# Seven half products for the eighth tile too, four matmuls handed to the next pair, and one of GpSimd's six differences as an adding transfer

## The chip, the cores and the metric

The kernel runs on one core of one Trainium2 chip. The metric is the device time of one execution in microseconds, as the median of several runs. An interval or a chance refers to that time. "The profile" is one execution recorded by the hardware profiler; its busy times, waits and timelines are of that execution alone.

## The reference

The task is a forward pass of a compressed interaction network. Three layers each form all products of two feature vectors, contract them with a weight, and hand half of the rows on.

```python
def _cin_forward(x, Ws, bs, fc_w, fc_b, split_half=True):
    x0 = x
    h = x
    xs = []
    n = len(Ws)
    for i in range(n):
        z = jnp.einsum('bfe,bge->bfge', x0, h)
        Bn, f0, fh, e = z.shape
        z = z.reshape(Bn, f0 * fh, e)
        y = jnp.einsum('oc,bce->boe', Ws[i], z) + bs[i][None, :, None]
        if split_half and i != n - 1:
            half = y.shape[1] // 2
            x_i, h = (y[:, :half, :], y[:, half:, :])
        else:
            x_i, h = (y, y)
        xs.append(x_i)
    pooled = jnp.sum(jnp.concatenate(xs, axis=1), axis=2)
    return pooled @ fc_w.T + fc_b
```

x is 1024 x 64 x 16 in float32, every layer has 128 output rows, and the result is 1024 numbers.

## The kernel before

The batch is cut into 32 chunks of 32 rows; a chunk has N = 512 columns (32 rows of 16 elements). The 64 x 64 products of a chunk are symmetric, so the kernel forms only the 16 tiles of 128 x 512 that cover each pair of features once. A block of four tiles with the same j (128 x 2048) is one product of VectorE: the chunk `xa` times a shifted copy of itself, `xb`, broadcast over the four. Fourteen such blocks, z0 to z13, are handed around by `take` and `used`: `take(uses)` takes the block that has been vacant longest, and a block becomes vacant when its uses are counted down. That happens while the program is written out, so each instruction's block is fixed, and a semaphore wait stands where a block is written again.

Each tile meets two weights of 64 columns, called h and q (`wh_all`, `wq_all`); the rest of the network is folded into them. A matmul of 64 output columns fills half the width of TensorE, so two of them, into the upper and the lower 64 partitions of PSUM, run side by side. Below, such a pair is called a row.

Chunks 6 to 31 are worked in 13 pairs (k = 3 to 15). In a pair the tiles with j = 0, 1 and those with j = 2, 3 of chunks a and b form a 2 x 2 matrix, the h and q weights of the two halves another, and their product is made by Winograd's scheme with seven half products instead of eight. The seven operands come from four kinds of blocks, each for j = 0 and 1:

- X (chunk a, low half), B21 (chunk a, high half) and B22 (chunk b, high half), which are products of VectorE in `w_product`;
- T3, a product too, of chunk b with the sum of two shifted copies, which `w_both` adds in PSUM;
- three differences that GpSimd forms in `w_mix` from these: T2 (from T3 and X), then T1, written over T3 (from B22 and T2), then T4, written over T2 (from T2 and B21). For j = 1 T2 is written over X from k = 4 on.

So there are six passes of GpSimd a pair. For j = 0 a pass covers four tiles (128 x 2048); for j = 1 it covers three (`slice(j, NI)`, 128 x 1536), because the first tile with j = 1, the eighth of each half, is left out of Winograd's scheme: `GROUPS` lacks (1, 0), each of the seven runs has seven matmuls, and the left-out tile is done with eight plain half matmuls, spread over `first_fill`, `second_fill`, `left_run` and `window`. A pair thus needs 7 x 7 + 8 = 57 half matmuls, and two more for the diagonal (`q_extra`).

`window` writes the order of TensorE's queue by hand as two columns which `zipped` interleaves: row by row one matmul of each. Column one has the X run into alpha, first fill, the T2 run, second fill, the T1 run; column two the T3 run into delta, the last pair's late run (B22 into its alpha), the B21 run into beta, the T4 run into delta. The fills hold what is left of the pair before: in `second_fill` the last one or two matmuls of its T4 run (`p["late"]`, by turns 1 and 2, 0 in the first pair). After a window come four small matmuls on 64 rows (`squares`).

The other engines' order is fixed by times in units of about a row: `make_pair` gives them for the ten VectorE operations and (`mixed`) GpSimd's six, `end_pair` for the final products of the pair before, `load_pair` for the loads on SyncE's queue. `at` collects them and everything is sorted by time at the end, so these numbers set only the order of each engine's queue; what then waits is up to semaphores. ScalarE copies the shifted chunks into PSUM (`second`), so that a VectorE product has one operand in PSUM, and keeps copies of alpha and delta (`snap_p1`, `snap_p7`, `snap_u2`) before further runs are added onto them. The run of T2 into alpha waits for `snap_p1`, and the run of T1 for `snap_u2`.

After 13 windows a final window adds the rest of the last pair and the kept chunks 2 and 3, and the sums are pooled and written out.

Of the kernel before, what the change touches and what calls it, by code (L numbers as in the profile page):

```python
# [38 lines left out]
AF = mybir.ActivationFunctionType  # L39
ALU = mybir.AluOpType  # L40
AX = mybir.AxisListType

F = 64
# [7 lines left out]
NI = 4  # L51
NJ = 4
NT = NI * NJ
# [8 lines left out]
NZ = 14  # L62
SPAN = 31
NPAIR = NCH // 2 - 3
GROUPS = [(j, i) for j in range(2) for i in range(NI) if (j, i) != (1, 0)]


@with_exitstack
def cin_kernel(ctx, tc, xra, xrb, wh, w0r, w1h, w2t, wx1, wx0, vec, out):
    nc = tc.nc  # L70
# [57 lines left out]


    w_all = const_tile("w_all", [128, NT, 128])  # L130
    ws = const_tile("ws", [128, 5, 2 * NI, F])
    va, vb, v0 = (const_tile(n, [128, F]) for n in ("va", "vb", "v0"))

    res = const_tile("res", [128, 128])
# [232 lines left out]
    for h in range(2):  # L367
        at = slice(32 * h, 32 * h + 32)
# [43 lines left out]
    for half, queue in enumerate((nc.sync, nc.scalar)):  # L412
        queue.dma_start(
            out=m_ap(0, 32 * half, [[row, F], [1, 32 * F]]), in_=m_rows[halves[half]]
# [5 lines left out]
        out=m_ap(64, 68, [[row, 4], [4 * F, 7], [1, 4 * F]]),  # L420
# [93 lines left out]
    def at(when, fn, *args, **flags):  # L514
        ops.append((when, len(ops), fn, args, flags))
# [104 lines left out]

    def w_run(p, out, w, name, start=False, at_t=0, order=GROUPS):
        return [
            (w_job, p, out, w, j * NI + i + at_t, name, start and n == 0)
            for n, (j, i) in enumerate(order)
        ]

    wh_all, wq_all = w_all[:, :, 0:64], w_all[:, :, 64:128]
    s1, s2, s3, s4, neg = (ws[:, n] for n in range(5))

    def w_product(p, c, j, name, uses, engine=nc.vector):  # L630
        p.setdefault(name, {})[j % 2] = b = take(uses)
# [6 lines left out]
        nc.vector.tensor_tensor(bank, bank, xbs[p["b"]][j], ALU.add)  # L638
        xbs[p["b"]][j] = bank

    def w_mix(p, j, out, in0, in1):
        p.setdefault(out, {})
        if j not in p[out]:
            p[out][j] = p["X"][j] if j and p["k"] > 3 else take(9 - 2 * j)
        o, x, y = p[out][j], p[in0][j], p[in1][j]
        tiles = slice(j, NI)
        nc.gpsimd.tensor_tensor(  # L647
            blocks[o][:, tiles], blocks[x][:, tiles], blocks[y][:, tiles], ALU.subtract
        )
        for b in (x, y):  # L650
            if b != o:
                used(b)
# [26 lines left out]
    def make_pair(t, p, when, mixed):  # L679
        a, b = p["a"], p["b"]  # L680
        for when, c, j, name, uses in (
            (when[0], b, 2, "B22", 5), (when[1], b, 0, None, 0), (when[2], b, 0, "T3", 9),
            (when[3], a, 0, "X", 5), (when[4], b, 3, "B22", 6), (when[5], b, 1, None, 0),
            (when[6], b, 1, "T3", 9), (when[7], a, 1, "X", 12 if p["k"] > 3 else 6), (when[8], a, 2, "B21", 5),
            (when[9], a, 3, "B21", 6),
        ):
            if name is None:
                at(t + when, w_both, p, j)
                continue
            if name == "B21" and j == 2 and p["k"] == 3:  # L690
                at(t + when, w_product, p, c, j, name, uses, engine=nc.gpsimd)
                continue
            if name != "T3":
                ahead = 3.3 if p["k"] > 4 and name == "B22" and j == 2 else 2.7
                if p["k"] == 3 and name == "X" and j == 1:
                    ahead = 9.1
                at(t + when - ahead, second, c, j)
            at(t + when, w_product, p, c, j, name, uses)
        for when, j, *names in zip(
            mixed, (0, 1, 0, 1, 0, 1), *zip(  # L700
                *(2 * (("T2", "T3", "X"),) + 2 * (("T3", "B22", "T2"),) + 2 * (("T2", "T2", "B21"),))
            )
        ):
            at(t + when, w_mix, p, j, *names)

    def first_fill(p):
        a = p["a"]
        return [
            (w_job, p, beta, wq_all, NI, "X"), (w_job, p, beta, wq_all, NT - NI, "B21"),
            (lambda: q_extra(a, va, p["beta"]),),  # L710
        ]

    def second_fill(p):
        return [
            (w_job, p, delta, wh_all, NI, "X"), (w_job, p, delta, wh_all, NT - NI, "B21"),
        ] + w_run(p, delta, neg, "T2")[7 - p["late"] :]

    def left_run(p, out, start=False):
        return [(w_job, p, out, neg, NI, "T3", start), (w_job, p, out, s4, NI, "B22")]

    def late_run(p, left=True):
        b = p["b"]
        return (left_run(p, alpha) if left else []) + w_run(p, alpha, s4, "B22") + [(lambda: q_extra(b, vb, p["alpha"]),)]

    def squares(p):
        a, b = p["a"], p["b"]
# [2 lines left out]
        v0x(b, "set")  # L729
        v0x(a, "set")  # L730

    def window(t, p, fill, late, pad=[], order=GROUPS[4:] + GROUPS[:4]):
        zipped(
            t,
            w_run(p, alpha, wq_all, "X", True, order=order) + fill[0] + w_run(p, alpha, s2, "T2")
            + fill[1] + w_run(p, alpha, s1, "T3")
            + [(w_job, p, alpha, wh_all, NI, "T3"), (w_job, p, alpha, s1, NI, "B22")],
            w_run(p, delta, s3, "T3", True) + late
            + w_run(p, beta, wq_all, "B21", True, 2 * NI)
            + pad + w_run(p, delta, neg, "T2")[: 7 - p["late"]],  # L740
        )
        at(t + 30.2, squares, p)
        at(t + 6.8, snap_p1, p)
        at(t + 6.9, snap_p7, p)
        at(t + 6.8 + len(fill[0]) + 7, snap_u2, p)

    def end_pair(t, p, whens):
        hb_, qa, uub, ha, uua, xv, add = whens
# [28 lines left out]
    def w_sums(m):  # L777
        h, q = w_all[:, 8 * m : 8 * m + 8, 0:64], w_all[:, 8 * m : 8 * m + 8, 64:128]
        if m:
            nc.gpsimd.tensor_tensor(ws[:, 3], q, ws[:, 1], ALU.subtract)  # L780
            nc.gpsimd.tensor_tensor(vb[halves[1]], va[halves[1]], w0ds[halves[1]], ALU.subtract)
            nc.scalar.activation(ws[:, 4], h, AF.Identity, scale=-1.0)
            nc.scalar.activation(ws[:, 4, NI], ws[:, 2, NI], AF.Identity, scale=-1.0)
            return
        nc.gpsimd.tensor_tensor(ws[:, 2], h, q, ALU.subtract)
        nc.gpsimd.tensor_tensor(ws[:, 1], ws[:, 0], q, ALU.add)
# [41 lines left out]
        at(34.5, factors, c)  # L828
    at(34.6, sums, 0, slice(0, 128), slice(0, 1))
    for c in (4, 5):  # L830
        at(T0 + 19.5, factors, c)
    at(T0 + 19.6, sums, 2, slice(0, 128), slice(0, 1))


    pairs = []
    for n in range(NPAIR):
        k = n + 3
        s = k % 2
        p = {
            "k": k, "A": halves[s], "O": halves[1 - s], "b": 2 * k + s, "a": 2 * k + 1 - s,  # L840
            "late": 1 + n % 2 if n else 0,
        }
        pairs.append(p)
        t = T0 + SPAN * n
        if n == 0:
            load_pair(t, p, -39.9, -33.3, -33.15, -27)
            make_pair(
                t, p, (-23.4, -20.7, -20.4, -17.8, -17.2, -16.8, -16.6, -7, -13.5, 3),
                (-14, -6.9, 7.2, 12.4, 16.4, 21.7),
            )  # L850
            left5 = [[(contract_half, 5, 3, i, n) for i in (2, 3)] for n in range(2)]
            window(
                t, p, ([left5[1][0], (q_extra, 4, va)], [left5[1][1]]),
                [left5[0][0], (q_extra, 5, va), None, None], [left5[0][1], None],
                GROUPS,
            )
        else:
            q = pairs[-2]
            load_pair(t, p, -34, -28, -27.8, -27.7)
            make_pair(  # L860
                t, p, (-21.4, -18.7, -18.4, -15.8, -12.2, -9.5, -6.1, -2, 1.6, 4.2),
                (-5, 2.8, 7.2, 12.4, 16.4, 21.7),
            )
            window(t, p, (first_fill(q), second_fill(q)), late_run(q))
            end_pair(t, q, (0.7, 11.7, 17.9, 22.3, 23.2, 24, 27.5))
# [109 lines left out]
    at(t + 11.6, end_gamma)  # L975
# [8 lines left out]
    at(t + 10.9, end_squares)  # L984
    at(t + 15, x_v0x, 1)
    at(t + 15.1, sums, 1, of=slice(1, 2))
    t += 25
# [98 lines left out]
```

## Time and profile before

| | |
|---|---|
| time, median of 3 runs | 459.09 us (458.66 to 459.91) |
| the profiled execution's own time | 458.84 us |
| its span, from first to last instruction | 457.0 us |
| TensorE clock granted | 1.000 |
| VectorE: tile products of a pair, each | 2280 ns |
| GpSimd: a difference over four tiles, over three | 4565 ns, 3468 ns |
| bytes moved by DMA | 86.04 MB |

Busy time is given per engine as time and share of the span. A group of instructions is given by its line in the kernel, its engine and what it writes and reads, with its number, its total time and the mean of one, and then the idle time of the engine just before, with the releaser. PE is TensorE, PEld its weight loads, DVE VectorE, ACT ScalarE, POOL GpSimd, SP SyncE. TensorE's float32 matmuls appear as two passes each, so the number of passes is twice the number of matmuls. A matmul's 592 ns in the records is its length from start to estimated end; the next one in the same column starts 428 ns after it.

### The profile page before, as it was taken

The page shows a single profiled execution, that of the slowest core. Times are in us where ns is not written, and L with a number is a line of the kernel's source. Part 1 is how long each engine was busy: PE and PEld are TensorE (multiplying, and loading weights), DVE is VectorE, ACT ScalarE, POOL GpSimd, SP SyncE. Part 2 cuts the span into 40 slices and gives each one's busy share as a digit, 9 for nine tenths or more (in the row PEclk, how much of TensorE's full clock was granted, in tenths as well). Part 3 has the DMA queues.
Part 4 walks back from the last instruction along what each step waited for, and adds up shares of the span by engine and source line. Part 5 has one row for each costly group of instructions (what it writes and reads, how often), then busy time and mean ns, then how long its engine had stood idle before and what let it go on. Part 6 is the DMA issues. An engine that isn't in the chain of part 4 may idle for free.

```text
span 457.0 us, 6105 instructions
## 1 busy us (share of the span) xinstructions
PE 451.5 (99%) x2328; PEld 163.8 (36%) x2328; DVE 393.6 (86%) x284; ACT 117.0 (26%) x216; POOL 367.8 (80%) x112
## 2 busy tenths in 40 slices
PE   7999999999999999999999999999999999999997
PEld 4565343332333333333333333333333333333345
DVE  4995499989898989989898998989899898979643
ACT  3162251241313123131312213131221312124011
POOL 5322788998998979799797979979797997979900
PEclk9999999999999999999999999999999999999999
DMA  8996998494739174563818365381836548250000
GB/s 294 416 309 147 345 375 341 144 307 134 254 94 313 31 260 143 183 221 121 283 36 269 133 205 198 114 299 35 276 116 205 199 136 290 70 184 23 24 0 2
DMA packets 32612, 86.04 MB, mean 188 GB/s; under 512 B 6116, under 2 KB 6788, under 8 KB 27656
## 3 DMA queue, kind: packets, MB, share of 16 engines
q1 hardware_dynamic: 31800, 84.70, 54.0%
q10 hardware_dynamic: 784, 0.95, 0.8%
q8 instruction: 18, 0.29, 0.3%
q14 instruction: 10, 0.08, 0.1%
HBM read 84.00 MB, written 1.64 MB: 187 GB/s over the span
## 4 chain that ended last, share of the span: by engine, by line
PE 97%; DMA 2%; SPq 0%; issue 0%; DVE 0%; ACT 0%; ACTq 0%
PE alpha L524 59%; PE delta L524 10%; PE beta L524 7%; PE acc L524 6%; PE acc L250 6%; PE q L524 3%; PE acc L268 3%; DMA z<-in_w0r 2%; PE y L524 1%; PE pm L384 0%; PE pv L357 0%; SPq L144 0%; PE xp L219 0%; PE hx L524 0%; PE pc L892 0%
## 5 line engine op out<-in xcount | busy, mean ns | idle before, releaser
L647 POOL TENSOR_TENSOR z<-z,z 128x2048 f32<-128x2048 f32 x78 | 310.4, 4017 | 31.2 <-PE alpha L524 31.2
L632 DVE TENSOR_TENSOR z<-xa,xp 128x2048 f32<-128x2048 f32 x103 | 232.6, 2280 | 15.3 <-POOL z L647 13.0
L524 PE MATMUL alpha<-z,ws 128*64 128x512 f32 x624 | 210.9, 592 | 0.0
L524 PE MATMUL delta<-z,ws 128*64 128x512 f32 x364 | 163.1, 594 | 0.0
L524 PEld LDWEIGHTS alpha<-z,ws 128*64 128x64 f32 x624 | 66.2, 137 | 110.4 <-issue 109.7
L552 ACT COPY xp<-xb 128x512 f32<-128x512 f32 x88 | 51.6, 588 | 209.3 <-DVE z L632 181.8
L524 PE MATMUL beta<-z,w_all 128*64 128x512 f32 x234 | 105.0, 593 | 0.0
L524 PE MATMUL alpha<-z,w_all 128*64 128x512 f32 x208 | 94.1, 595 | 0.2
L524 PEld LDWEIGHTS delta<-z,ws 128*64 128x64 f32 x364 | 48.7, 137 | 15.0 <-issue 13.5
L240 DVE TENSOR_TENSOR z<-xa,xp 128x2048 f32<-128x2048 f32 (+2 forms) x23 | 45.1, 2002 | 10.2 <-ACT xp L552 8.9
L524 PEld LDWEIGHTS alpha<-z,w_all 128*64 128x64 f32 x208 | 27.5, 137 | 62.2 <-issue 51.8
L240 POOL TENSOR_TENSOR z<-xa,xb 128x2048 f32<-128x2048 f32 x6 | 27.2, 4554 | 18.5 <-DMA xb<-in_xrb 18.5
L524 PEld LDWEIGHTS beta<-z,w_all 128*64 128x64 f32 x234 | 31.4, 137 | 14.6 <-issue 14.5
L250 PE MATMUL acc<-z,w_all 128*64 128x256 f32 x256 | 29.2, 382 | 2.1 <-DVE z L240 1.9
L524 PE MATMUL acc<-z,w_all 128*64 128x512 f32 (+1 forms) x96 | 29.4, 594 | 0.0
L524 PE MATMUL delta<-z,w_all 128*64 128x512 f32 x52 | 24.4, 592 | 0.0
L250 PEld LDWEIGHTS acc<-z,w_all 128*64 128x64 f32 x256 | 18.0, 137 | 14.4 <-DVE z L240 3.7
L292 DVE TENSOR_REDUCE acc<-uu 128x64 f32<-128x1024 f32 (+2 forms) x19 | 19.6, 1035 | 0.2
L638 DVE TENSOR_TENSOR xp<-xp,xb 128x512 f32<-128x512 f32 x26 | 18.2, 699 | 0.8
L655 ACT COPY snap<-alpha 64x512 f32<-64x512 f32 x13 | 7.5, 581 | 40.6 <-PE delta L524 40.6
L524 PE MATMUL y<-e,v 64*64 64x512 f32 x64 | 17.0, 612 | 0.0
L524 PE MATMUL q<-z,w_all 128*64 128x384 f32 (+1 forms) x128 | 16.9, 381 | 0.0
(117 smaller groups left out, 320.6 us busy)
## 6 DMA issues: line engine op xcount, KB each, us to landing
xa<-in_xra SPq DMA_DIRECT2D x32, 1024.0 KB, 4.6
xb<-in_xrb SPq DMA_DIRECT2D x128, 256.0 KB, 6.7
e<-in_xra SPq DMA_DIRECT2D x28, 128.0 KB, 4.3
xx<-in_xra SPq DMA_DIRECT2D x28, 128.0 KB, 2.5
z<-in_w2t SPq DMA_DIRECT2D x2, 1024.0 KB
z<-in_wx SPq DMA_DIRECT2D x2, 1024.0 KB, 7.8
z<-in_w1h SPq DMA_DIRECT2D x1, 1024.0 KB
xa<-in_xra SPq DMA_DIRECT2D x3, 256.0 KB
```

What stands on the lines that cost most here:

```text
L240: engine.tensor_tensor(blocks[zs[c, j]][:, at, :], xas[c][:, at, :], xbs[c][j].unsqueeze(1).to_broadcast([128, last - first, N]), ALU.mult,)
L250: nc.tensor.matmul(accs[c][halves[n]], w_all[:, t, 0:64], blocks[zs[c, j]][:, i, n * H2 : (n + 1) * H2], start=(t == 0), stop=(j == last a ...
L268: nc.tensor.matmul(accs[c][halves[1 - c % 2]], w_all[:, t, 64:128], blocks[zs[c, j]][:, i, :], start=(t == 0), stop=False, skip_group_chec ...
L292: nc.vector.tensor_reduce(acc[rows, of, k, half], uu[rows, of if at is None else at, E * half.start : E * half.stop].rearrange("p k (b e) ...
L524: nc.tensor.matmul(out, w, rhs, start=start, stop=stop, skip_group_check=True)
L552: nc.scalar.copy(bank, xbs[c][j])
L632: engine.tensor_tensor(blocks[b], xas[c], xbs[c][j].unsqueeze(1).to_broadcast([128, NI, N]), ALU.mult)
L638: nc.vector.tensor_tensor(bank, bank, xbs[p["b"]][j], ALU.add)
L647: nc.gpsimd.tensor_tensor(blocks[o][:, tiles], blocks[x][:, tiles], blocks[y][:, tiles], ALU.subtract)
L655: nc.scalar.copy(snaps[0][p["O"]], alpha(p))
```

## The change

`GROUPS` has all eight (j, i), so each of the seven runs has eight matmuls and the plain ones go, with `left_run`. All passes of GpSimd cover four tiles. The T2 pass with j = 1 is cut in two halves of two tiles each. T2 is now X - T3 instead of T3 - X, so that T1 is B22 + T2 and T4 is T2 + B21: the signs of two weight blocks turn around, `neg` goes, and the T4 run takes `wh_all` itself. The T4 pass with j = 1 is no pass of GpSimd any more: GpSimd's queue issues a transfer that adds B21's block onto T2's block, both in SBUF, 1 MiB each. The four T4 matmuls that read this block are taken out of the pair's own window (`LATE = 4`): two go into the first fill and two into the second fill of the next pair's window. `p["late"]` goes. The uses of the blocks, the times of GpSimd's passes and of the snapshots, and the order of the final window follow. No load is changed.

```diff
-GROUPS = [(j, i) for j in range(2) for i in range(NI) if (j, i) != (1, 0)]
+GROUPS = [(j, i) for j in range(2) for i in range(NI)]
+LATE = 4
...
-    s1, s2, s3, s4, neg = (ws[:, n] for n in range(5))
+    s1, s2, s3, s4 = (ws[:, n] for n in range(4))
...
-    def w_mix(p, j, out, in0, in1):
+    def w_mix(p, j, out, in0, in1, first=0, last=NI):
         p.setdefault(out, {})
         if j not in p[out]:
-            p[out][j] = p["X"][j] if j and p["k"] > 3 else take(9 - 2 * j)
+            p[out][j] = p["X"][j] if j and p["k"] > 3 else take(9)
         o, x, y = p[out][j], p[in0][j], p[in1][j]
-        tiles = slice(j, NI)
-        nc.gpsimd.tensor_tensor(
-            blocks[o][:, tiles], blocks[x][:, tiles], blocks[y][:, tiles], ALU.subtract
-        )
+        if in1 == "B21" and j:
+            nc.gpsimd.dma_start(out=blocks[o], in_=blocks[y], accum_op=ALU.add)
+        else:
+            nc.gpsimd.tensor_tensor(
+                *(blocks[b][:, first:last] for b in (o, x, y)),
+                ALU.subtract if in1 == "T3" else ALU.add,
+            )
+        if last < NI:
+            return
...
-            (when[3], a, 0, "X", 5), (when[4], b, 3, "B22", 6), (when[5], b, 1, None, 0),
-            (when[6], b, 1, "T3", 9), (when[7], a, 1, "X", 12 if p["k"] > 3 else 6), (when[8], a, 2, "B21", 5),
-            (when[9], a, 3, "B21", 6),
+            (when[3], a, 0, "X", 5), (when[4], b, 3, "B22", 5), (when[5], b, 1, None, 0),
+            (when[6], b, 1, "T3", 9), (when[7], a, 1, "X", 13 if p["k"] > 3 else 5), (when[8], a, 2, "B21", 5),
+            (when[9], a, 3, "B21", 5),
...
-        for when, j, *names in zip(
-            mixed, (0, 1, 0, 1, 0, 1), *zip(
-                *(2 * (("T2", "T3", "X"),) + 2 * (("T3", "B22", "T2"),) + 2 * (("T2", "T2", "B21"),))
-            )
+        t2, t1, t4 = ("T2", "X", "T3"), ("T3", "B22", "T2"), ("T2", "T2", "B21")
+        for when, j, names in zip(
+            mixed, (0, 1, 1, 0, 1, 1, 0), (t2, (*t2, 0, 2), (*t2, 2), t1, t1, t4, t4)
         ):
             at(t + when, w_mix, p, j, *names)
 
+    def p4_run(p):
+        return w_run(p, delta, wh_all, "T2", at_t=2 * NI)
+
     def first_fill(p):
-        a = p["a"]
-        return [
-            (w_job, p, beta, wq_all, NI, "X"), (w_job, p, beta, wq_all, NT - NI, "B21"),
-            (lambda: q_extra(a, va, p["beta"]),),
-        ]
+        return [(lambda: q_extra(p["a"], va, p["beta"]),)] + p4_run(p)[-LATE : -LATE // 2]
 
     def second_fill(p):
-        return [
-            (w_job, p, delta, wh_all, NI, "X"), (w_job, p, delta, wh_all, NT - NI, "B21"),
-        ] + w_run(p, delta, neg, "T2")[7 - p["late"] :]
-
-    def left_run(p, out, start=False):
-        return [(w_job, p, out, neg, NI, "T3", start), (w_job, p, out, s4, NI, "B22")]
-
-    def late_run(p, left=True):
-        b = p["b"]
-        return (left_run(p, alpha) if left else []) + w_run(p, alpha, s4, "B22") + [(lambda: q_extra(b, vb, p["alpha"]),)]
+        return p4_run(p)[-LATE // 2 :]
+
+    def late_run(p, out=alpha, first=0, last=2 * NI):
+        jobs = w_run(p, out, s4, "B22", out is gamma)[first:last]
+        return jobs if last < 2 * NI else jobs + [(lambda: q_extra(p["b"], vb, p["alpha"]),)]
...
-    def window(t, p, fill, late, pad=[], order=GROUPS[4:] + GROUPS[:4]):
+    def window(t, p, fill, late, pad=[], order=GROUPS[NI:] + GROUPS[:NI]):
         zipped(
             t,
             w_run(p, alpha, wq_all, "X", True, order=order) + fill[0] + w_run(p, alpha, s2, "T2")
-            + fill[1] + w_run(p, alpha, s1, "T3")
-            + [(w_job, p, alpha, wh_all, NI, "T3"), (w_job, p, alpha, s1, NI, "B22")],
-            w_run(p, delta, s3, "T3", True) + late
-            + w_run(p, beta, wq_all, "B21", True, 2 * NI)
-            + pad + w_run(p, delta, neg, "T2")[: 7 - p["late"]],
+            + fill[1] + w_run(p, alpha, s1, "T3"),
+            w_run(p, delta, s3, "T3", True) + late + w_run(p, beta, wq_all, "B21", True, 2 * NI)
+            + pad + p4_run(p)[:-LATE],
         )
...
-            nc.scalar.activation(ws[:, 4], h, AF.Identity, scale=-1.0)
-            nc.scalar.activation(ws[:, 4, NI], ws[:, 2, NI], AF.Identity, scale=-1.0)
+            nc.scalar.activation(ws[:, 1], ws[:, 1], AF.Identity, scale=-1.0)
...
-                (-14, -6.9, 7.2, 12.4, 16.4, 21.7),
+                (-14, -6.9, -6.8, 7.2, 12.4, 17.6, 17.5),
...
-                (-5, 2.8, 7.2, 12.4, 16.4, 21.7),
+                (-5, 1.6, 3.6, 7.2, 12.4, 18.6, 18.5),
...
-        first_fill(q) + left_run(q, gamma, True) + second_fill(q)
+        first_fill(q) + second_fill(q) + late_run(q, gamma, 0, 2)
         + [(end_q, 3, m, 0) for m in range(NT)] + [(end_extra, 3, 0)],
-        [(end_q, 2, m, 0) for m in range(3)] + late_run(q, False)
+        [(end_q, 2, m, 0) for m in range(3)] + late_run(q, first=2)
         + [(end_q, 2, m, 0) for m in range(3, NT)] + [(end_extra, 2, 0)],
```

More of the change, by code (lines that the diff above doesn't have):

```diff
@@ L130, in cin_kernel @@
     w_all = const_tile("w_all", [128, NT, 128])
-    ws = const_tile("ws", [128, 5, 2 * NI, F])
+    ws = const_tile("ws", [128, 4, 2 * NI, F])
     va, vb, v0 = (const_tile(n, [128, F]) for n in ("va", "vb", "v0"))
@@ L735, in window @@
             w_run(p, alpha, wq_all, "X", True, order=order) + fill[0] + w_run(p, alpha, s2, "T2")
-            + fill[1] + w_run(p, alpha, s1, "T3")
-            + [(w_job, p, alpha, wh_all, NI, "T3"), (w_job, p, alpha, s1, NI, "B22")],
-            w_run(p, delta, s3, "T3", True) + late
-            + w_run(p, beta, wq_all, "B21", True, 2 * NI)
-            + pad + w_run(p, delta, neg, "T2")[: 7 - p["late"]],
+            + fill[1] + w_run(p, alpha, s1, "T3"),
+            w_run(p, delta, s3, "T3", True) + late + w_run(p, beta, wq_all, "B21", True, 2 * NI)
+            + pad + p4_run(p)[:-LATE],
         )
         at(t + 30.2, squares, p)
-        at(t + 6.8, snap_p1, p)
-        at(t + 6.9, snap_p7, p)
-        at(t + 6.8 + len(fill[0]) + 7, snap_u2, p)
+        at(t + 7.3, snap_p1, p)
+        at(t + 7.8, snap_p7, p)
+        at(t + 7.3 + len(fill[0]) + 8, snap_u2, p)
     def end_pair(t, p, whens):
@@ L830, in cin_kernel @@
     for c in (4, 5):
-        at(T0 + 19.5, factors, c)
-    at(T0 + 19.6, sums, 2, slice(0, 128), slice(0, 1))
+        at(T0 + 21, factors, c)
+    at(T0 + 21.1, sums, 2, slice(0, 128), slice(0, 1))
     pairs = []
@@ L840, in cin_kernel @@
             "k": k, "A": halves[s], "O": halves[1 - s], "b": 2 * k + s, "a": 2 * k + 1 - s,
-            "late": 1 + n % 2 if n else 0,
         }
@@ L974, in cin_kernel @@
     end_pair(t, q, (0.7, 4.5, 13.8, 8.5, 9, 9.5, 14.5))
-    at(t + 11.6, end_gamma)
+    at(t + 10.5, end_gamma)
     at(t - 0.1, new_ends)
@@ L978, in cin_kernel @@
         t,
-        first_fill(q) + left_run(q, gamma, True) + second_fill(q)
+        first_fill(q) + second_fill(q) + late_run(q, gamma, 0, 2)
         + [(end_q, 3, m, 0) for m in range(NT)] + [(end_extra, 3, 0)],
-        [(end_q, 2, m, 0) for m in range(3)] + late_run(q, False)
+        [(end_q, 2, m, 0) for m in range(3)] + late_run(q, first=2)
         + [(end_q, 2, m, 0) for m in range(3, NT)] + [(end_extra, 2, 0)],
     )
-    at(t + 10.9, end_squares)
+    at(t + 9.9, end_squares)
     at(t + 15, x_v0x, 1)
```

## The prediction

> **What bounds the kernel now.** I read the busy table first, then the chain that ended last, then the groups with shapes kept apart, then the timelines of TensorE, GpSimd, VectorE and the DMA queue over one pair of the steady state, and last the waits.
>
> ```profile
> span 457.0 us, 6105 instructions
> PE 451.5 (99%) x2328; PEld 163.8 (36%) x2328; DVE 393.6 (86%) x284; ACT 117.0 (26%) x216; POOL 367.8 (80%) x112
> ...
> PE 97%; DMA 2%; SPq 0%; issue 0%; DVE 0%; ACT 0%; ACTq 0%
> ```
>
> TensorE is full and is 97% of the chain, so a matmul that goes is worth its time, as long as VectorE and GpSimd keep up. How close they are is seen in the groups and timelines (start, length, engine, line; idle time before it and its releaser in brackets).
>
> ```profile
> 226.24 6.02 PE alpha L524 x29
> 252.41 6.01 PE alpha L524 x29
> 279.33 6.01 PE alpha L524 x29
> ...
> L647 POOL TENSOR_TENSOR z<-z,z 128x2048 f32<-128x2048 f32 x39 | 178.0, 4565 | 0.0
> L647 POOL TENSOR_TENSOR z<-z,z 128x1536 f32<-128x1536 f32 x39 | 135.3, 3468 | 31.2 <-PE alpha L524 31.2
> ...
> L240 POOL TENSOR_TENSOR z<-xa,xb_gps 128x1024 f32<-128x1024 f32 x1 | 2.3, 2347 | 4.2 <-DMA xa<-in_xra 4.2
> ...
> 88.14 23.84 POOL L647 TENSOR_TENSOR z<-z,z 128x1536 f32<-128x1536 f32 x6
> 220.31 23.88 POOL L647 TENSOR_TENSOR z<-z,z 128x1536 f32<-128x1536 f32 x6 [3.03 <-PE alpha L524]
> ...
> 223.87 2.29 DVE L632 TENSOR_TENSOR z<-xa,xp 128x2048 f32<-128x2048 f32 x1 [1.07 <-POOL z L647]
> 232.33 0.69 DVE L675 SCALAR_TENSOR_TENSOR uu<-alpha,snap 64x512 f32<-64x512 f32 x1
> 241.29 2.27 DVE L632 TENSOR_TENSOR z<-xa,xp 128x2048 f32<-128x2048 f32 x1
> ...
> 243.62 0.64 PE L524 MATMUL alpha<-z,w_all 128*64 128x512 f32 x1
> 270.54 0.64 PE L524 MATMUL alpha<-z,w_all 128*64 128x512 f32 x1
> ...
> 240.26 0.33 SPq L144 DMA_DIRECT2D xa<-in_xra  x1
> 240.69 3.19 SPq L158 DMA_DIRECT2D xb<-in_xrb  x6
> ```
>
> The same place in three windows lies 26.17 and then 26.92 us apart, and so on alternately to the end (mean 26.54): windows of 29 and 30 rows. A row is two half matmuls side by side, each of two passes, started every 0.428 us: 0.857 us a row (the difference of the windows, 0.75, is less; I come back to it). GpSimd works 3 x 4.565 + 3 x 3.468 = 24.1 us a pair and idles 2.3 to 3.0, always for the X run that frees the block its second difference overwrites. VectorE's eight products (2.28 us) and small operations are some 25.0 us, and its last product (241.29 + 2.27 = 243.56) ends when the next window's first matmul starts (243.62). So three engines stand within 2.5 us of each other.
>
> **What the Trainium skill says.** "DMA: Bandwidth & Descriptors", section on the anatomy of a GpSimd DMA: about 2.0 us fixed plus bytes over 436 GB/s; for 1 MiB an estimate of 4.4 us. "Collectives: The Full Stack", section on the bandwidth ceiling: an adding transfer goes at half a copy's rate, since it reads two sources; estimate 2.0 + 2 x 2.4 = 6.8 us. "Perfetto Trace Analysis", section on the GpSimd DMA instruction: GpSimd writes the descriptors itself, and the transfer's end is not in the instruction's span. No run yet shows any of these; before has no GpSimd DMA. "GPSIMD Engine Reference", section 3.1, gives 4497 ns for a 128x2048 f32 addition; the trace's 4565 agrees.
>
> **The change, part by part.** All against the profiled execution, 458.84 us (span 457.0 and 1.8 around it); the median 459.09 is 0.25 above, which I add at the end.
>
> 1. Matmuls. Per pair seven runs of eight (56) instead of seven of seven and eight plain ones (57); with the two extras 58 instead of 59. The order of TensorE's queue confirms it: 986 matmuls become 973. Written into two columns, before has 28 and 29 rows (second window), then 30/30 and 29/29 by turns; after has 29/29 always. Six windows (third, fifth, ... thirteenth) lose a row. The second loses only half of its unpaired row, which I count nothing. The first keeps 27 rows: the four jobs handed on come back in the next. In the final window each column loses one full-width job: one row, 0.86 us.
>
> 2. What a lost row is worth. A 29-row window took 26.17 us on the chain; TensorE alone would need 29 x 0.857 + 1.22 for the four squares (269.32 to 270.54) = 26.07. The rest is VectorE's: its uu from alpha waits for the late extra in row 16 (started 232.33, 14.82 after the window's start at 217.51), and from there nine operations without a gap end with the product that starts the next window. Row 16 and these nine stay as they are, so I take 26.17 for every window: 6 x (26.92 - 26.17) = 4.5 us. Bounds: 4.2 (0.05 more on each) to 5.1 (26.07).
>
> 3. GpSimd. Six passes of 2048 and 1536 become four of 2048 and two of 1024: 4 x 4.565 + 2 x 2.347 = 22.95 us, plus D, the time it writes descriptors. Period 26.17, so D up to 3.2 us is free. D: below, nothing; above, the whole fixed 2.0 us; I take 1.0. By place: the first half may start after two rows of X (1.94 us into the window), the differences end at 6.6, 11.2, 15.7 and 20.3; they are wanted at rows 15, 21, 25 and 25, thus 12.9, 18.0, 21.4 and 21.4. The tightest margin is 1.1 us, where before it was 1.8 (18.8 against row 24). So nothing here, in the steady state.
>
> 4. The adding transfer comes behind the fourth difference in GpSimd's queue, 20.3 us into the window. Queued behind it is the next pair's first difference, not wanted until row 11 of the next window. Who waits for the transfer: the four handed-over matmuls, at row 9 of the next window (26.17 + 7.7 = 33.9), and VectorE: the B21 product of j 1 now reuses the block the transfer reads, and in return the first product of the next pair no longer waits for GpSimd (the 1.07 above goes). That B21 product comes 3.0 us into the next window; VectorE can lose 1.2 us more before uu, whose wait for row 16 swallows it. So the landing is due at 26.17 + 3.0 + 1.2 = 30.4, that is 10.1 us after issue. Alone it takes 4.4 to 6.8 (estimates above); but from 24.7 us into the window the loads issued at 240.26 and 240.69 (2.5 MB) fill the DMA engines until about 32. An estimate for the slow bound: begin at 21.3, 3.4 of 4.8 us done by 24.7, the other 1.4 at half rate, 1 us receipt: landed at 28.5, 8.2 after issue. I take no stall. The loads, if slowed by the same 2.4 to 4.8 us of traffic, have room: those issued at 240.26 are used from 12 us into the next window on, the other group a whole window after issue.
>
> 5. First window. GpSimd runs without a gap from 88.14, and TensorE took up the fourth difference at 104.09, just when 3.47 + 4.57 + 3.47 + 4.57 had passed. Now it is 2 x 2.35 + 3 x 4.57 = 18.4, at 106.4, with five rows left instead of seven: 106.4 + 4.3 against 104.1 + 6.0, with small overlaps of the passes 0.5 us later.
>
> 6. Final window. The last handed-over jobs stand in row 1, 26.17 + 0.86 - 20.3 = 6.7 us after issue, no loads beside it: nothing with 4.4, 0.1 with 6.8, perhaps 1 with a large D. I take 0.2.
>
> 7. Nothing: the weight block negated on ScalarE instead of a second one written (ScalarE 26% busy, before the windows), the moved snapshots (each still within the three fill rows ahead of the run that waits for it), the later factors.
>
> Sum: 458.84 - 4.5 - 0.86 + 0.5 + 0.2 = 454.2; with 0.25 for the median 454.4.
>
> **The rivals.** (a) The transfer lands late (slower). VectorE waits at the B21 product in every one of twelve windows, and each microsecond beyond 10.1 costs 12. From 10.5 the gain is gone; 11.5 us would give 454.4 + 12 x 1.4 = 471, 11.0 gives 465. For it: the load burst, and that no trace shows the adding rate. Against: my slow bound is 8.2. Chance 0.15. (b) GpSimd becomes the bound, since D is beyond 3.2 us: period 22.95 + D, with D = 4 it is 26.95, so 454.4 + 12 x 0.78 = 463.8. For it: it stands 3.2 us from the bound already. Against: the skill calls most of the fixed time receipt, not GpSimd's. Chance 0.07. (c) The lost row only turns into waiting on VectorE, 0.4 us more in each window by B21 or the T4 wait: 454.4 + 12 x 0.4 = 459.2, no change. Against: its one new wait has 1.2 us of cover. Chance 0.05. That the count doesn't fall is excluded by the order.
>
> **How the numbers follow.** Forecast 0.73, with its own range 452.8 (26.07 everywhere, no cost in the first and final window) to 456.5 (0.1 us more in each window and 1 at the end). The same case holds 0.05, rivals (a) and (b) 0.22. To leave no more than 2 in 10 out, the range goes from 452.8 to 461.0, through (c) and the mild part of (a) and (b). What this measurement can tell from no change is about 0.3%, 1.4 us: faster 0.73, same 0.05, slower 0.22.
>
> **What would show it.** Right: windows evenly 26.1 to 26.2 apart; VectorE's third wait for GpSimd gone and no DMA as releaser of its products; GpSimd idle 1 to 3 us a pair for X; the first window about 0.5 us longer. Wrong: products of line 633 waiting for a DMA from z to z, GpSimd's passes without a gap over a window, or windows above 26.5.

## The result, and the profile after

The changed kernel takes 464.28 us (median of 4 runs, 463.19 to 464.71). Before, run on the same chip, takes 459.5 us. The ratio is 1.0103, interval 1.0079 to 1.0127: slower by 1%, where 454.4 us and a gain of 1% had been forecast. The profiled spans are 457.0 us before and 462.9 us after.

From the page after: the span, the busy times, the granted clock in 40 slices, and the shares of the chain that ended last.

```profile
span 462.9 us, 6067 instructions
PE 448.8 (97%) x2302; PEld 161.4 (35%) x2302; DVE 393.6 (85%) x284; ACT 116.7 (25%) x215; POOL 364.4 (79%) x125
...
PEclk9999999999799999999999999999999999999999
...
PE 78%; DVE 10%; DMA 5%; issue 5%; SPq 0%; POOL 0%; ACT 0%; POOLq 0%; DVEq 0%; ACTq 0%
```

TensorE has less to do than before (448.8 us instead of 451.5), as planned, and yet the span grew. Its share of the chain fell from 97% to 78%, DMA rose from 2% to 5%, and one slice of the clock shows 7. Most of the 15% of DVE and issue lies in every other window of the steady state, where the chain runs through VectorE for some 11 us; these windows did not grow, as the next lines show. What is new is the DMA share and the slice of the clock. Lines of the chain after (start, length, what), and the first and last window of the same stretch before:

```profile
106.67 8.17 DMA z<-z
...
129.60 5.58 PE alpha L525 x26
...
208.17 5.18 PE alpha L525 x25
...
234.45 5.58 PE alpha L525 x26
...
260.60 5.18 PE alpha L525 x25
...
286.88 5.58 PE alpha L525 x26
...
417.87 5.58 PE alpha L525 x26
...
428.41 9.11 DMA z<-z
```

```profile
120.06 6.01 PE alpha L524 x29
...
411.69 6.01 PE alpha L524 x29
```

The runs of T2 into alpha mark the windows. They lie 26.28, 26.15 and 26.28 us apart here. Over the eleven periods from the second window to the thirteenth they take 417.87 - 129.60 = 288.3 us; before it was 411.69 - 120.06 = 291.6. The steady state thus gained 3.4 us. The two transfers on the chain are the first and the last of thirteen, and around them the gain is lost. Timeline after, GpSimd, VectorE and TensorE (start, length, engine, line; idle time before it and its releaser in brackets), and then the first matmul of the second window before:

```profile
106.67 0.96 POOL L648 DMA_DIRECT2D z<-z  x1
107.43 4.78 POOL L650 TENSOR_TENSOR z<-z,z 128x2048 f32<-128x2048 f32 x1
...
107.67 2.29 DVE L633 TENSOR_TENSOR z<-xa,xp 128x2048 f32<-128x2048 f32 x1
114.97 2.29 DVE L633 TENSOR_TENSOR z<-xa,xp 128x2048 f32<-128x2048 f32 x1 [5.00 <-DMA z<-z]
...
117.31 1.11 PE L525 MATMUL alpha<-z,w_all 128*64 128x512 f32 x1 [5.81 <-DVE z L633]
118.22 1.06 PE L525 MATMUL alpha<-z,w_all 128*64 128x512 f32 x1
...
122.48 0.68 PE L525 MATMUL alpha<-z,w_all 128*64 128x512 f32 x1
...
226.81 18.27 POOL L650 TENSOR_TENSOR z<-z,z 128x1024 f32<-128x1024 f32 x5 [2.69 <-PE alpha L525]
244.99 0.85 POOL L648 DMA_DIRECT2D z<-z  x1
...
255.24 4.49 DVE L633 TENSOR_TENSOR z<-xa,xp 128x2048 f32<-128x2048 f32 x2 [1.35 <-DMA z<-z]
...
437.57 0.64 PE L525 MATMUL delta<-z,w_all 128*64 128x512 f32 x1 [2.21 <-DMA z<-z]
```

```profile
111.26 0.64 PE L524 MATMUL alpha<-z,w_all 128*64 128x512 f32 x1
```

At the start: the first pair's transfer is issued at 106.67. VectorE's next product but one, the X product with j = 1 of the second pair, takes the block that this transfer reads, so it waits 5.00 us, and TensorE, whose second window begins with that product, idles 5.81 us. The window begins at 117.31 instead of 111.26, which is 6.05 us (0.46 of it was there when the first window began, at 86.22 instead of 85.76). Then the passes follow each other at 0.85 us instead of 0.43, until 122.48. Those six steps took 5.17 us instead of 2.55 to 2.6, another 2.6 us. In the middle (226.81 to 255.24) GpSimd still idles 2.69 us for the X run, and VectorE waits 1.35 us for a transfer. It does so in five windows from the seventh on, for 0.17 to 1.35 us each. At the end the last pair's handed-over matmuls wait 2.21 us for the last transfer.

So the span's difference of +5.9 us is 6.05 + 2.6 at the start, -3.4 in eleven periods, and +0.6 for the rest: the thirteenth and the final window with the rows saved there, the last wait and the wind-up. The landings are seen in the view of the transfer's line and in the DMA queues (packets, MB, share of 16 engines' span; q0 holds GpSimd's transfers, q1 the loads):

```profile
DMA to landing us min/median/max: 8.2/9.1/10.2
```

```profile
q1 hardware_dynamic: 31800, 84.70, 50.7%
q0 software_dynamic: 1872, 13.63, 16.6%
```

A transfer lands 8.2 to 10.2 us after issue, not 4.4 to 6.8. It occupies the 16 engines for 0.166 x 462.9 / 13 = 5.9 us, while a load costs 0.507 x 462.9 / 84.7 = 2.8 us per MB, so 2.9 us for the 1.05 MB of one transfer.

### The profile page after: what moved, and what is told of

Same layout as the page of the kernel before. It is cut to its first block, busy times and chain, and to the rows that moved or that the text cites. A ratio compares the mean times of both kernels' runs of the same rounds, so it can differ in the third digit from the quotient of the medians.

```text
span 462.9 us, 6067 instructions
## 1 busy us (share of the span) xinstructions
PE 448.8 (97%) x2302; PEld 161.4 (35%) x2302; DVE 393.6 (85%) x284; ACT 116.7 (25%) x215; POOL 364.4 (79%) x125
## 4 chain that ended last, share of the span: by engine, by line
PE 78%; DVE 10%; DMA 5%; issue 5%; SPq 0%; POOL 0%; ACT 0%; POOLq 0%; DVEq 0%; ACTq 0%
PE alpha L525 48%; PE delta L525 8%; PE acc L525 6%; PE acc L251 6%; DVE z L633 5%; DMA z<-z 4%; PE q L525 3%; PE acc L269 3%; PE beta L525 2%; DMA z<-in_w0r 2%; DVE acc L293 1%; DVE uu L289 1%; DVE uu L681 1%; DVE delta L678 1%; DVE xp L639 1%
## 5 line engine op out<-in xcount | busy, mean ns | idle before, releaser
L650 POOL TENSOR_TENSOR z<-z,z 128x2048 f32<-128x2048 f32 (+1 forms) x78 | 299.7, 3871 | 38.3 <-PE alpha L525 38.0
L633 DVE TENSOR_TENSOR z<-xa,xp 128x2048 f32<-128x2048 f32 x103 | 232.4, 2280 | 10.5 <-DMA z<-z 8.0
L525 PE MATMUL alpha<-z,ws 128*64 128x512 f32 x624 | 219.1, 592 | 0.0
L525 PEld LDWEIGHTS alpha<-z,ws 128*64 128x64 f32 x624 | 69.1, 137 | 117.7 <-issue 116.6
L525 PE MATMUL delta<-z,w_all 128*64 128x512 f32 x208 | 95.6, 593 | 2.7 <-DMA z<-z 2.2
L525 PE MATMUL delta<-z,ws 128*64 128x512 f32 x208 | 94.6, 609 | 0.0
L525 PE MATMUL beta<-z,w_all 128*64 128x512 f32 x208 | 91.7, 593 | 0.0
L241 POOL TENSOR_TENSOR z<-xa,xb 128x2048 f32<-128x2048 f32 x6 | 27.5, 4637 | 19.9 <-DMA xb<-in_xrb 19.9
L525 PEld LDWEIGHTS delta<-z,w_all 128*64 128x64 f32 x208 | 28.3, 137 | 34.7 <-issue 30.2
L525 PEld LDWEIGHTS delta<-z,ws 128*64 128x64 f32 x208 | 28.1, 140 | 0.0
L525 PEld LDWEIGHTS beta<-z,w_all 128*64 128x64 f32 x208 | 27.8, 137 | 0.0
L251 PEld LDWEIGHTS acc<-z,w_all 128*64 128x64 f32 x256 | 18.1, 137 | 13.8 <-DVE z L241 2.9
L664 ACT ACTIVATE snap<-alpha,vs 64x512 f32<-64x512 f32 x13 | 8.9, 683 | 53.8 <-PE alpha L525 53.8
```

The costliest lines, as they stand in the source:

```text
L241: engine.tensor_tensor(blocks[zs[c, j]][:, at, :], xas[c][:, at, :], xbs[c][j].unsqueeze(1).to_broadcast([128, last - first, N]), ALU.mult,)
L251: nc.tensor.matmul(accs[c][halves[n]], w_all[:, t, 0:64], blocks[zs[c, j]][:, i, n * H2 : (n + 1) * H2], start=(t == 0), stop=(j == last a ...
L525: nc.tensor.matmul(out, w, rhs, start=start, stop=stop, skip_group_check=True)
L633: engine.tensor_tensor(blocks[b], xas[c], xbs[c][j].unsqueeze(1).to_broadcast([128, NI, N]), ALU.mult)
L650: nc.gpsimd.tensor_tensor(*(blocks[b][:, first:last] for b in (o, x, y)), ALU.subtract if in1 == "T3" else ALU.add,)
L664: nc.scalar.activation(snaps[1][p["O"]], alpha(p), AF.Identity, bias=bh1[p["A"]])
```

## The experiments

Each expectation names its theory and the rivals. All diffs are against the changed kernel unless another is named.

**A different block for one product.** `take` hands out the block that has been vacant longest. In the second pair the X product with j = 1 gets the next one instead, so it no longer meets the first transfer. All later products get other blocks by this too.

```diff
     def w_product(p, c, j, name, uses, engine=nc.vector):
+        if p["k"] == 4 and name == "X" and j == 1:
+            vacant.append(vacant.pop(0))
         p.setdefault(name, {})[j % 2] = b = take(uses)
```

> Edit: before the X product with j 1 of the second pair (k = 4) takes its block, the longest vacant block, the one the first pair's adding transfer still reads, is moved to the end of the list; nothing else. Theory 1 (the loss at the start is one block: that product waits 5.0 us for the transfer, TensorE idles 5.8 us behind it and then runs 2.6 us slower): the second window starts within 0.3 us of the end of the first, at about 111.5 instead of 117.3, its first matmuls start 0.43 us apart, and the time falls by 8.0 to 8.7 us, to 455.6 to 456.3. Rival (the transfers load all windows): all windows keep what they have, the time stays within 1 us of 464.3.

Measured: 457.45 us (median of 20 runs), ratio to before 0.9963 (0.9953 to 0.9973), 6.8 us less than the changed kernel. Chain of this kernel:

```profile
110.47 2.29 DVE z L635
...
421.28 9.10 DMA z<-z
```

The product starts at 110.47 instead of 114.97, the window at 112.81, the clock of the profiled execution is 1.000, and the later windows stay 26.15 and 26.27 us long. From the first window's start to the second's it now takes 26.0 us, where it took 31.1 in the changed kernel and 25.5 before. VectorE still holds the second window up a little: it waited 1.1 and 1.5 us for ScalarE's copies at the first window's factors, where it had not waited before, and the chain runs through these factors. The wait of the last window stays. Less came back than forecast: the twenty executions lie between 456.21 and 458.86 us, the ten with a granted clock of 1.000 at a median of 456.6 and the ten with 0.996 at 458.2. Where the latter lost time no trace shows; a possible place is seen in the experiment with zero weights below. One block's reuse cost more than the whole change gained.

**The last pair without a transfer.** The last pair's sixth difference is a pass of GpSimd again.

```diff
-        if in1 == "B21" and j:
+        if in1 == "B21" and j and p["k"] < 15:
```

> Edit: the last pair's fourth difference with j 1 is a GpSimd pass again (4.6 us) instead of the transfer. Theory 1 (the end loses only the wait of row 1 for the landing, 437.57 against 435.2): the pass ends at 433.0, the wait is gone, the time falls by 2.2 to 2.6 us, to 461.7 to 462.1. Rival (what bounds the end is VectorE or ScalarE, and TensorE's wait is covered): below 1 us.

Measured: 461.6 us, ratio 1.0063 (1.0043 to 1.0082), 2.7 us less than the changed kernel. The chain has no transfer at the end any more. The last pair's matmuls want the result 6.8 us after issue (435.19 - 428.41), and no window follows that could hide a landing of 9.1 us. A pass of 4.57 us is sooner done.

**The transfer one place earlier in GpSimd's queue**, ahead of the other T4 pass, so that it lands earlier.

```diff
-                (-14, -6.9, -6.8, 7.2, 12.4, 17.6, 17.5),
+                (-14, -6.9, -6.8, 7.2, 12.4, 17.5, 17.6),
-                (-5, 1.6, 3.6, 7.2, 12.4, 18.6, 18.5),
+                (-5, 1.6, 3.6, 7.2, 12.4, 18.5, 18.6),
```

> Edit: in all pairs the transfer is issued before the fourth difference of j 0, not behind it. Theory 1 (only two landings matter, the first pair's and the last's): the transfers are issued 3.7 us earlier and the difference ends 0.8 us later. The first landing is at 110.2 to 111, the product waits at most 1 us, TensorE's idle time falls from 5.8 to below 2.5 us; the last landing comes before the final window; together 454 to 457 us. Rival (the fourth difference has no margin to give): TensorE waits for GpSimd in each window at row 25, up to 0.6 us, twelve times, so 458 to 464.

Measured: 466.6 us, ratio 1.0186 (1.0156 to 1.0217), with the version without a transfer (466.15, below) the slowest. Timeline of this kernel, GpSimd, and then its chain:

```profile
114.29 13.74 POOL L650 TENSOR_TENSOR z<-z,z 128x1024 f32<-128x1024 f32 x4 [2.03 <-PE alpha L525]
129.35 0.88 POOL L648 DMA_DIRECT2D z<-z  x1 [1.32 <-issue]
129.96 9.36 POOL L650 TENSOR_TENSOR z<-z,z 128x2048 f32<-128x2048 f32 x2
```

```profile
121.93 5.58 PE alpha L525 x26
...
149.12 5.58 PE alpha L525 x26
...
176.29 5.58 PE alpha L525 x26
```

The start was cured (VectorE's wait fell to 0.31 us), but every window is now 27.2 us long. The transfer writes T2's block, which TensorE's T2 run reads, and at the new place that run is only just over: its last matmul here ends at 128.80. The trace names that run as what the transfer waited for in one of thirteen cases and nothing ("issue") in twelve, so this cause is likely and not shown. GpSimd stands still for 1.32 us with T4's other pass queued behind, and TensorE's T4 run, which needs that pass, is late in all windows (13.8 us of idle time of its weight loads in 13 waits). A wait in a queue costs what stands behind it, in this case a microsecond in each of twelve windows against 8.6 us once. Neither the theory nor the rival had expected so much.

**Work for TensorE while it waits.** Six matmuls with zero weights, which add nothing to the first pair's delta, stand ahead of the second window, to keep the engine from idling.

```diff
+    def idle_fill(p):
+        mm(delta(p), zeros[:, 0:64], blocks[p["T2"][0]][:, 0, :])
...
+            if n == 1:
+                for m in range(6):
+                    at(t - 0.3, idle_fill, q)
```

> Edit: six matmuls with a weight of zeros, which add nothing to delta of the first pair, stand in TensorE's queue after the first window, in the 5.8 us in which it idles. Theory 1 (the slow start of the second window, matmuls 0.85 us apart for about 5 us, comes from the idle time before it): with TensorE busy the first matmuls are 0.43 us apart, TensorE starts the second window at the same place, about 117.3, and the time falls by 2.3 to 2.8 us, to 461.5 to 462.0. Rival (the slow stretch has another cause): it stays, and the time is within 0.5 us of 464.3.

Measured: 461.99 us, ratio 1.0069 (1.0042 to 1.0096), 2.3 us less. Timeline of this kernel, VectorE and TensorE, at the second window and at the last wait:

```profile
114.15 2.29 DVE L633 TENSOR_TENSOR z<-xa,xp 128x2048 f32<-128x2048 f32 x1 [5.06 <-DMA z<-z]
...
116.49 0.64 PE L525 MATMUL alpha<-z,w_all 128*64 128x512 f32 x1 [0.55 <-DVE z L633]
116.97 0.59 PE L525 MATMUL alpha<-z,w_all 128*64 128x512 f32 x1
...
117.40 0.59 PE L525 MATMUL alpha<-z,w_all 128*64 128x512 f32 x1
...
434.12 0.79 PE L525 MATMUL delta<-z,w_all 128*64 128x512 f32 x1 [2.25 <-DMA z<-z]
...
434.70 1.06 PE L525 MATMUL delta<-z,w_all 128*64 128x512 f32 x1
...
435.56 1.06 PE L525 MATMUL delta<-z,w_all 128*64 128x512 f32 x1
```

VectorE waits as long as ever, but the next passes start 0.48 and 0.43 us apart. So the slow passes after the stall are a second price of the idle time itself, 2.6 us by the timelines and 2.3 by the medians. The Trainium skill, "TensorE: Matmul & The Clock Gate", part 1, says that the clock falls to half after an idle window of about 3.4 us and comes back after about as much sustained work. Half rate agrees (0.85 against 0.43), and the slow stretch was longer here, 5.2 us. The idle time need not be that long: in this profile the last wait, 2.25 us, is followed by slow passes too (0.86 us apart), and the end takes 1.7 us longer than in the changed kernel, where after 2.21 us of waiting the passes stay 0.43 us apart. What decides between the two is not shown.

**Both cures together**: the first and the second diff.

> Edit: both single edits together, the block of the second pair's X product and the last pair's GpSimd pass. Theory 1 (the change loses in two places that have nothing to do with each other, and gains in every window): the two gains of 6.8 and 2.7 us add up, 454.6 to 455.2, which is 4 us faster than before. Rival (one wait takes the other's place): less than 8 us together, above 456.

Measured: 454.29 us (454.0 to 454.33), ratio 0.9898 (0.9883 to 0.9913). The two gains add up, 10.0 us together against 6.8 + 2.7 = 9.5 one by one, so neither wait takes the other's place. With both gone the kernel takes what had been forecast for the change as it was. In part that is chance: the forecast had 0.7 us for these two places, and its windows were a little short (26.17 us where 26.21 were measured in the changed kernel).

**VectorE's uu one place later**, on top of the last: uu from alpha goes behind the product that followed it, so its wait for the late extra no longer holds that product up.

```diff
-            end_pair(t, q, (0.7, 11.7, 17.9, 22.3, 23.2, 24, 27.5))
+            end_pair(t, q, (0.7, 11.7, 18.9, 22.3, 23.2, 24, 27.5))
```

> Edit: as the kernel with both edits, and in each window VectorE forms the pair's fourth product (B22 with j 1) before the uu from alpha, not behind it. Theory of the prediction (a window is 26.2 us and not TensorE's 26.07, since that uu waits about 1 us for row 16 and the operations behind it end as the next window starts): the wait is covered, windows are 26.05 to 26.1 apart, and the time falls by 1.0 to 1.7 us against the kernel with both edits. Rival (TensorE is the whole bound, the rest lies in its own start of a window): windows stay at 26.2, less than 0.4 us.

Measured: 452.6 us (451.71 to 453.73), ratio 0.9864 (0.9843 to 0.9885), 1.7 us less than without. Chain of this kernel:

```profile
199.36 5.58 PE alpha L525 x26
...
225.42 5.58 PE alpha L525 x26
...
251.49 5.58 PE alpha L525 x26
```

The windows are now 26.06 and 26.07 us long, which is TensorE's own length as the prediction worked it out. So the 0.1 us on top of it came from VectorE, whose uu waits for row 16.

**The first pairs' factors later**, on top of that: the waits for ScalarE's copies.

```diff
-        at(T0 + 21, factors, c)
-    at(T0 + 21.1, sums, 2, slice(0, 128), slice(0, 1))
+        at(T0 + 25, factors, c)
+    at(T0 + 25.1, sums, 2, slice(0, 128), slice(0, 1))
```

> Edit: as the one with uu later, and in the first window the factors of chunks 4 and 5 come after the pair's T3 product with j 1 in VectorE's queue. Theory (of the start's loss about 1 us is left, since VectorE waits 1.1 and 1.5 us for ScalarE's snapshots ahead of the product that opens the second window): that product ends before 111, the second window starts at 111.5 to 112, and the time falls by 0.6 to 1.2 us against the one with uu later, to about 452.5. Rival (the fourth difference, up late from GpSimd, holds the first window anyway): less than 0.3 us.

Measured: 451.65 us (450.71 to 453.57, 5 runs), ratio 0.9835 (0.9818 to 0.9851), the fastest version. The two waits are gone from VectorE's timeline. Its interval overlaps that of the version before it, so the step of 0.95 us is likely but not sure. The profiled execution, with a span of 451.7 us, is one that came into the first window about 2 us late: the same product of VectorE starts at 91.72 there and at 89.66 in the version before. From there to the T2 run of the second window it needs 31.0 us against 31.5, so by the profiles the step is worth 0.5 us.

**No transfer at all.** All six differences are passes of GpSimd, with the handed-over matmuls and everything else of the change kept.

```diff
-        if in1 == "B21" and j:
+        if in1 == "B21" and j and False:
```

> Edit: the changed kernel, with all six differences of a pair as GpSimd passes and no adding transfer; the hand-over and the seven runs of eight stay. Theory (the transfer is needed, since GpSimd would be the bound: 5 x 4.6 + 2 x 2.37 = 27.7 us a pair): windows are 27.6 to 27.9 apart, TensorE or VectorE waits for GpSimd in each, no loss at start and end; 12 x 1.5 more in the windows and 9 to 10 less at the ends give 470 to 474. Rival (GpSimd's passes shorten where the next engine waits): below 464.

Measured: 466.15 us (463.74 to 468.51), ratio 1.0157 (1.0119 to 1.0196). Chain shares of this kernel's page and two windows of its chain:

```profile
PE 53%; POOL 28%; issue 12%; DVE 5%; DMA 1%; SPq 0%; ACT 0%; ACTq 0%; POOLq 0%
```

```profile
282.22 5.18 PE alpha L525 x25
...
336.72 5.18 PE alpha L525 x25
```

GpSimd is now 28% of the chain, and two windows take 54.50 us, 27.25 each: 5 x 4.57 + 2 x 2.35 = 27.5 less small overlaps of its passes. So GpSimd does become the bound without the transfer. The expected 470 to 474 was too high, since its passes enter the chain window after window only from 168 us on, a few windows in, and the pace is a little under the sum. Against the version with both cures the twelve transfers are worth 466.15 - 454.29 = 11.9 us by the medians (the four executions here lie between 463.74 and 468.51) and 9.4 by the profiled spans (461.9 and 452.5).

**A copy in place of the adding transfer.** Only `accum_op` is left out, so the T2 term is missing from four tiles of T4. Bytes, queue and waits are the same.

```diff
-            nc.gpsimd.dma_start(out=blocks[o], in_=blocks[y], accum_op=ALU.add)
+            nc.gpsimd.dma_start(out=blocks[o], in_=blocks[y])
```

> The changed kernel with its adding transfer made a plain copy (the T2 term is left out of the four tiles of T4 with j = 1); everything else as it is, bytes and queue too. It measures the term of the sum that was mis-sized, the landing. Theory 1 (the adding itself costs: it goes at half a copy's rate): engine time per transfer falls from 5.9 us to that of a load's MB, 2.8 to 3.0, the landing of the last one, which has no load beside it, from 9.1 to 6.0 to 6.5 us; the wait at the end goes (2.2 us), VectorE's wait at the start falls from 5.0 to 2 to 2.5, and with the idle time of TensorE the stretch at half clock becomes shorter: 457 to 460 us in all. Theory 2 (the fixed part of a GpSimd transfer inside SBUF is what was too small, not the rate): the landing stays at 8 to 9 us, the waits stay at 4 to 5 and 1.5 to 2.2 us, and the time at 463 to 464 us.

Measured, in one run: 454.91 us, span 453.1, where before took 458.2 on the same chip. Timeline of this kernel, GpSimd and VectorE, the view of the transfer's line and the DMA queues:

```profile
105.54 0.72 POOL L648 DMA_DIRECT2D z<-z  x1
...
110.46 2.29 DVE L633 TENSOR_TENSOR z<-xa,xp 128x2048 f32<-128x2048 f32 x1 [0.86 <-PE y L525]
```

```profile
DMA to landing us min/median/max: 4.8/5.4/6.7
```

```profile
q1 hardware_dynamic: 31800, 84.70, 53.3%
q0 software_dynamic: 1872, 13.63, 9.5%
```

The landing falls from 9.1 to 5.4 us and the time on the DMA engines from 5.9 to 0.095 x 453.1 / 13 = 3.3 us per transfer. The wait at the end is gone. At the start VectorE's wait falls from 5.00 to 0.86 us. The trace puts this rest down to TensorE, but the first transfer lands 4.8 us after its issue, at 110.3, just before the product starts, and the same product had no wait with the block exchanged; so it is most likely still the transfer. TensorE's idle time there falls from 5.81 to 2.39 us, and its passes then start 0.43 to 0.48 us apart, with no slow stretch. More came back than theory 1 had asked for, since the copy lands sooner than it expected; with one execution the size is rough. The windows stay 26.14 and 26.28 us long, exactly as with the adding transfer. So in the steady state the slow landing cost nothing. What the copy leaves out changes the result, so it is no way to make the kernel faster.

## Why the prediction was wrong

It forecast 454.4 us, with a loss of 0.5 in the first window and 0.2 in the final one. The profiled span is 10.5 us above the forecast's (454.2 - 1.8 = 452.4): 8.1 at the start, 2.1 in the thirteenth and final window, 0.4 in the periods between. (The lower end of the forecast's own range, 26.07 us in all twelve windows and no cost at the ends, comes to 452.5 by its numbers and not to 452.8; nothing rests on it.)

- **Step 5, first window: failed.** It looked at TensorE and GpSimd (the fourth difference and the rows left), not at the block that VectorE takes next. That question had been put in step 4, but for a pair of the steady state, where the B21 product reuses the transfer's source 3 us into the next window and has cover. In the second pair, X with j = 1 reuses it at once and has none: VectorE was ready at 109.96, 3.3 us after issue. Even the estimate of 4.4 to 6.8 for the landing would have made VectorE wait 1 to 3.5 us there. Exchanging the block gave 6.8 us back, the wait and the slow passes behind it together. The slow clock after the stall was no term of the sum at all; the matmuls that filled the idle time put it at 2.3 to 2.6 us. The 0.5 us that the step did count are not the loss: from the first window's start to its four small matmuls TensorE took 24.2 us, and 24.5 before.
- **Step 4, the landing: mis-sized.** The forecast took 4.4 to 6.8 us alone and 8.2 at worst beside loads. Measured are 8.2 to 10.2, and 9.1 for the last transfer, which has only two loads of 128 KB beside it. The upper estimate had used the Trainium skill, "Collectives: The Full Stack", section on the bandwidth ceiling, which says that the reduce step of a collective runs at half the rate of a copy because it reads two sources; the forecast carried this over to a transfer within one core. The trace agrees roughly (5.9 against 3.3 us on the engines, a factor of 1.8). Two terms were too low: a copy takes 3.3 us on the engines, not 2.4, and beside the engine time the adding transfer needs 3.2 us (9.1 - 5.9), not 2.0. For the copy the fixed part of 2.0 fits (5.4 - 3.3 = 2.1).
- **Step 4, the consequence: right in the steady state.** The landing was due at 10.1 us after issue, and the transfers come in just by then. VectorE waits 0.17 to 1.35 us at the B21 product in five windows, and the wait for row 16 swallows it, as the step said: behind the wait of 1.35 us the uu starts without one, where it else waits 0.94. Rival (a), one late transfer in every window, did not come: the copy gives the same windows.
- **Step 6, final window: failed by the same size.** Matmuls 6.7 us after issue were to wait 0.1 at 6.8; with 9.1 the wait is 2.21, and the pair without a transfer gave back 2.7.
- **Steps 1 and 2, the rows: right.** 2302 passes instead of 2328, and a mean window of 26.21 us where 26.17 was taken; the version with uu later shows that TensorE alone needs the 26.07 of the lower bound.
- **Step 3, GpSimd: right.** The issue holds it for 0.84 us where 1.0 was taken, and the transfer is issued 20.2 us into a window, where 20.3 was forecast. Rival (b) did not come; the run without a transfer shows how long a window is when GpSimd is the bound and makes all six differences, 27.25 us.
- **Step 7: nearly right.** The later factors cost VectorE two new waits in the first window, 1.0 and 1.5 us; in the changed kernel the transfer hid them, and once the block is exchanged, moving the factors is worth 0.5 to 1.0 us, which is not sure.

The forecast's rivals were all taken from the steady state. The loss was in none of them: it occurs once at each end, and it outweighs the gain of all the windows between.

## What to carry to other kernels

When buffers are handed out while the program is written, a new reader of a buffer changes who waits for whom in every pair separately. Follow the first and the last pair through by hand, where the pattern isn't yet the one of the steady state and nothing covers a wait. A transfer like this one can take work off a full engine at no cost where neither its result nor its source is needed for about 10 us; where one of them is needed at once, leave the work on the engine.

## What the runs showed of the hardware

- An adding transfer of 1 MiB inside SBUF, issued by GpSimd, took 8.2 to 10.2 us to land, the same bytes as a copy 4.8 to 6.7. It kept the DMA engines busy for 5.9 and 3.3 us, a load of the same size from HBM for 2.9 us. GpSimd itself was held 0.84 us for the adding one and 0.57 for the copy.
- After 5.8 us without a matmul TensorE ran 5.2 us at half rate, so that the stall cost 8.6 us in all; six matmuls with zero weights in the gap took the half rate away, not the wait. After waits of 2.21, 2.23, 2.25 and 2.39 us in four profiles the passes were slow once, behind the one of 2.25.
- The median landing of the 1 MiB loads was 4.6 us before and 5.8 in the version without a transfer, 9.5 beside the adding transfers and 6.9 beside the copies. In the windows VectorE, GpSimd and TensorE waited for none of these loads.
